# A list scheduler's rules set anew: who holds the port of VectorE and GpSimd, how long dependent operations wait, how long operations last

## The chip, the cores and the metric

The kernel runs on one core of a Trainium2 chip. The core's engines work side by side, each through its own queue in order: TensorE (PE in the profile; its weight loads are PEld), VectorE (DVE), ScalarE (ACT), GpSimd (POOL), and SyncE (SP), which issues the DMAs. The metric is the device time of one execution in microseconds; lower is better. Three runs of the kernel before took 2602.37, 2603.43 and 2603.91 us; the median is 2603.43 us.

## The reference

The input is `x`, 128 graphs of 128 nodes with 256 features in float32, and an adjacency matrix `adj` of 128x128 for each graph. Four layers follow each other, and each ends in `x = layernorm(x + layer(x, adj))` over the features.

Layer 0 is a gated graph network of three steps. In each, a message is formed and summed over the neighbours, and a gated recurrent unit (GRU) takes it in:

```
m = h @ weight[i];  aggr = A^T @ m
r = sigmoid(i_r + h_r);  z = sigmoid(i_z + h_z);  n = tanh(i_n + r * h_n)
h = (1 - z) * n + z * h
```

Here `i_*` are the three parts of `aggr @ w_ih.T + b_ih` and `h_*` those of `h @ w_hh.T + b_hh`. Layers 1 to 3 are graph attention: `Wh = x @ W.T`, `e[i,j] = leaky_relu(Wh[i].a1 + Wh[j].a2, 0.2)`, masked by `adj`, a softmax over `j`, and the result times `Wh`. In layer 2 a node without neighbours gives zero.

## The kernel before, in words

**Tiling.** Four graphs form a group (`G = 4`), so that a tile of 128 partitions holds 512 columns; there are 32 groups. For each group `gru` (L534) records the operations of layer 0 and `gat` (L666) those of the three attention layers. The messages' weights are multiplied into the GRU's input weights, so a step is: sum over the neighbours on PE (L566), evict from PSUM, then the gate products (L508). These use Strassen's scheme with seven products in place of eight: `strassen` (L491) issues the products into three PSUM accumulators of the kind `gate`; ACT copies the intermediate ones out (L574, L578, L581) and DVE adds the parts (`add`, L513). What the scheme needs as moving operands are sums and differences of halves of the hidden state and of the aggregate; `sums` (L468, recorded at L478) makes four of them for each operand, 768 in all, on DVE or on POOL. ACT takes the sigmoids as tanh (L592) and the tanh (L621); DVE combines (L608, L612, L615, L618, L628, L631), and one subtraction (L626) may run on DVE or POOL.

In attention, DVE forms the scores as products with an accumulated row sum (L677), PE turns them into a row (L689), POOL spreads the row over the partitions (`partition_broadcast`, L696), DVE adds the mask and takes the maximum (L712), ACT applies the leaky rectifier (L716) and the exponential (L733), with tiny DVE operations of 128x4 between them (L722, L725, L729). PE transposes the result (L744), it is scaled or evicted (L749 on DVE, L753 on ACT), PE forms the two products (L774, L785), and DVE normalizes and adds the input (L791). ACT squares for the layernorm (L452), further tiny DVE operations follow (L456, L461, L463), POOL raises a 128x4 tile to the power -0.5 (`power`, L425), and ACT scales at the very end (L798). The last four groups make the scores' row on PE (L706) in place of L689 and L696. Where data is transposed by DMA (`turned`, L387), ACT or DVE takes the two halves of each float apart (`APART`, L402) and puts them together again (`TOGETHER`, L397 on ACT, L301 on DVE).

**What sets the order.** Nothing is issued while the operations are recorded. `plan.op` notes each with the engines that may run it and a duration for each, what it reads and writes, and a priority. `Plan.order` (L93) then runs a list scheduler over planned time. An operation becomes ready on an engine once all it depends on is done, plus a delay (`release`, L121 to L126): the producer's `LATENCY` if it ran on another engine, with `MARGIN` of 300 ns more if the consumer is PE; 60 ns on the same engine, 0 on PE. Among the ready operations of an idle engine the one with the lowest priority number goes first. Buffers are slots in pools (`k2` 28, `k4` 18, five `gate` and three `bank` accumulators in PSUM, and so on), and an operation whose buffers have no free slot waits.

**The port.** The scheduler has one resource beside engines and buffers: a port that DVE and POOL share. An operation names in `port` the engines on which it takes it; it then waits until the port is free and holds it for its planned duration. With `BOTH` it takes it on either engine; the default is `("POOL",)`, so every operation that runs on POOL takes it, and a DVE operation takes it only if marked. Of DVE and POOL the one whose first ready operation has the lower priority number is served first (`older`, L152).

The list that the scheduler returns is then issued as it stands. On the chip no planned time holds anything up: an instruction runs when those before it on its engine are done and its inputs are there.

Of the kernel before, what the change touches and what calls it, by code (L numbers as in the profile page):

```python
# [13 lines left out]
ALU = mybir.AluOpType  # L14
AX = mybir.AxisListType

P = 128
# [32 lines left out]
class Plan:  # L50
# [5 lines left out]
    LATENCY = {"PE": 250, "ACT": 220, "DVE": 200, "POOL": 250, "SP": 4000}  # L56
# [11 lines left out]
    def op(self, engines, fn, reads=(), writes=(), prio=0, lag=0, port=("POOL",), start=0, room=()):  # L68
# [24 lines left out]
    def order(self):  # L93
        import heapq
        for o in self.ops:
            o.missing = len(o.deps)
            o.at = {}
            for d in o.deps:
                d.users.append(o)
# [21 lines left out]
        def release(o):  # L121
            for e in o.engines:
                margin = self.MARGIN if e == "PE" else 0
                when = max([t + (margin + self.LATENCY[e2] if e2 != e else 0 if e == "PE" else 60) for e2, t in o.at.items()],
                           default=0)
                heapq.heappush(arrived, (max(when, o.earliest), o.prio, e, o))  # L126
# [4 lines left out]
        while len(done) < len(self.ops):  # L131
# [20 lines left out]
            older = ready["POOL"] and ready["DVE"] and ready["POOL"][0] < ready["DVE"][0]  # L152
            for e in ("PE", "ACT", "SP") + (("POOL", "DVE") if older else ("DVE", "POOL")):
# [51 lines left out]
def adj_resnorm_kernel(  # L205
# [98 lines left out]
    EVICT = {"ACT": 490, "DVE": 600}  # L304
    APART = {"ACT": 960, "DVE": 615}
    TOGETHER = {"ACT": 1075, "DVE": 615}
# [54 lines left out]
    def score_weights(l, prio):  # L361
# [6 lines left out]
        for k in range(KC):  # L368
            st, mv = Buf("st", 6), Buf("mv", G, 2)
            plan.op({"DVE": 330}, lambda e, k=k, st=st: nc.vector.bn_stats(T(st), T(gwT)[:, l, k, :]),  # L370
                    reads=[(gwT, l)], writes=[st], prio=prio)
            plan.op({"DVE": 110}, lambda e, st=st, mv=mv: nc.vector.bn_aggr(T(mv)[:, 0, :], T(st)),
                    reads=[st], writes=[mv], prio=prio)
            plan.op({"DVE": 330}, lambda e, k=k, mv=mv: nc.vector.tensor_scalar(
                T(gwT)[:, l, k, :], T(gwT)[:, l, k, :], T(mv)[:, 0, 0:1], None, op0=ALU.subtract),
                reads=[mv, (gwT, l)], writes=[(gwT, l)], prio=prio)
# [10 lines left out]
    def turned(src, keys, dst, prio):  # L387
# [15 lines left out]
        plan.op({"SP": 1200}, lambda e: nc.sync.dma_start_transpose(  # L403
# [4 lines left out]
    def transposed(src, src_of, prio):  # L408

        res = []  # L410
        for c in range(KC):
# [5 lines left out]
            plan.op({"PE": 440}, fn, reads=[src], writes=[b_], prio=prio)  # L417
# [4 lines left out]
    def power(ve, prio):  # L422

        rstd = Buf("v", G)
        plan.op({"POOL": 1035}, lambda e: nc.gpsimd.tensor_tensor(T(rstd), T(ve), neghalf, ALU.pow),  # L425
                reads=[ve], writes=[rstd], prio=prio)
        return rstd

    def layernorm(y, dst, prio):
        mv, ve, shift = Buf("mv", G, 2), Buf("v", G), Buf("v", G)  # L430
        for b in range(G):
            st = Buf("st", 6)
            plan.op({"DVE": 330}, lambda e, b=b, st=st: nc.vector.bn_stats(T(st), T(y)[:, b, :]),
                    reads=[(y, b)], writes=[st], prio=prio)
            plan.op({"DVE": 110}, lambda e, b=b, st=st: nc.vector.bn_aggr(T(mv)[:, b, :], T(st)),
                    reads=[st], writes=[(mv, b)], prio=prio)
        plan.op({"DVE": 100}, lambda e: nc.vector.tensor_scalar(T(ve), T(mv)[:, :, 1], EPS, None, op0=ALU.add),
                reads=[(mv, b) for b in range(G)], writes=[ve], prio=prio)
        rstd = power(ve, prio)
        plan.op({"DVE": 100}, lambda e: nc.vector.scalar_tensor_tensor(  # L440
            T(shift), T(mv)[:, :, 0], -1.0, T(rstd), op0=ALU.mult, op1=ALU.mult),
            reads=[(mv, b) for b in range(G)] + [rstd], writes=[shift], prio=prio)
        for b in range(G):
            plan.op({"ACT": 415}, lambda e, b=b: nc.scalar.activation(  # L444
# [3 lines left out]
    def deviation(y, before, prio):  # L448

        ss, ve = Buf("v", G), Buf("v", G)  # L450
        for b in range(G):
            plan.op({"ACT": 415}, lambda e, b=b: nc.scalar.activation(  # L452
                next(nobody[0]), T(y)[:, b, :], AF.Square, accum_out=T(ss)[:, b:b + 1]),
                reads=[(y, b)], writes=[(ss, b)], prio=prio)
        if before is None:
            plan.op({"DVE": 100}, lambda e: nc.vector.tensor_scalar(  # L456
                T(ve), T(ss), 1.0 / D, EPS, op0=ALU.mult, op1=ALU.add),
                reads=[(ss, b) for b in range(G)], writes=[ve], prio=prio)
        else:
            eps = Buf("v", G)  # L460
            plan.op({"DVE": 100}, lambda e: nc.vector.tensor_scalar(T(eps), T(before), EPS, None, op0=ALU.mult),  # L461
                    reads=[before], writes=[eps], prio=prio)
            plan.op({"DVE": 100}, lambda e: nc.vector.scalar_tensor_tensor(  # L463
                T(ve), T(ss), 1.0 / D, T(eps), op0=ALU.mult, op1=ALU.add),
                reads=[(ss, b) for b in range(G)] + [eps], writes=[ve], prio=prio)
        return ve

    def sums(ms, prio):  # L468
# [5 lines left out]
        for j, (a, b, reads) in enumerate((  # L474
                (second, first, [ms[0]]), (fourth, part(0), [ms[1], (t, 0)]), (fourth, second, ms),
                (part(1), third, [ms[1], (t, 1)]))):
            plan.op({"POOL": 720, "DVE": 350}, lambda e, j=j, a=a, b=b: (
# [13 lines left out]
    def strassen(gates, kept, prio):  # L491
# [7 lines left out]
        def product(dst, m, first, *room):  # L499
# [10 lines left out]
            plan.op({"PE": 432 * len(todo)}, fn, reads=list(keys), writes=[dst], prio=prio, room=room)  # L510

        def add(b_, part, o, j):
            plan.op({"DVE": 630}, lambda e: nc.vector.tensor_add(  # L513
# [20 lines left out]
    def gru(g, stage):  # L534
# [20 lines left out]
        for i in range(STEPS):  # L555
# [4 lines left out]
            for c in range(KC):  # L560
# [6 lines left out]
                plan.op({"PE": 4 * 222}, fn, reads=[am, xs if h is None else h[c]], writes=[b_], prio=prio, room=[a_])  # L567
# [5 lines left out]
            def whole(dst, src, c):  # L573
                plan.op({"ACT": 500}, lambda e: nc.scalar.copy(T(dst), T(src)),  # L574
                        reads=[src], writes=[(dst, 0), (dst, 1)], prio=prio)

            def halves(dst, src, c):
                plan.op({"ACT": 370}, lambda e: nc.scalar.activation(  # L578
                    T(dst)[:, 0:H], T(src)[:, 0:H], AF.Identity, bias=bhn[:, c:c + 1]),
                    reads=[src], writes=[(dst, 0)], prio=prio)  # L580
                plan.op({"ACT": 260}, lambda e: nc.scalar.copy(T(dst)[:, H:GN], T(src)[:, H:GN]),  # L581
# [5 lines left out]
            for c in range(KC):  # L587
# [6 lines left out]
                for gt in range(2):  # L594
                    if c == 0:
                        plan.op({"ACT": 630}, lambda e, gt=gt, o=o, tanh=tanh: tanh(gt, 0, GN, lambda: T(o)[:, gt, :]),
                                reads=[(o, 0), (o, 1)], writes=[(o, 2 + gt)], prio=prio)
                    else:
                        plan.op({"ACT": 365}, lambda e, gt=gt, tanh=tanh, rz=rz: tanh(
# [4 lines left out]
                if c == 1:  # L604
                    plan.op({"ACT": 370}, lambda e, v=v, nn=nn: nc.scalar.activation(  # L605
                        T(v)[:, 0, 0:H], T(nn[2])[:, 0:H], AF.Identity, bias=bhn[:, 1:2]),
                        reads=[nn[2]], writes=[(v, 0)], prio=prio)
                plan.op({"DVE": 620}, lambda e, o=o, v=v: nc.vector.scalar_tensor_tensor(  # L608
                    T(v)[:, 0, :], T(o)[:, 0, :], 1.0, T(v)[:, 0, :], op0=ALU.add, op1=ALU.mult),
                    reads=[(o, 2), (v, 0), (v, 1)], writes=[(v, 2)], prio=prio, port=BOTH)  # L610
                if c == 0:
                    plan.op({"DVE": 620}, lambda e, v=v: nc.vector.tensor_add(T(v)[:, 0, :], T(v)[:, 1, :], T(v)[:, 0, :]),  # L612
                            reads=[(v, 2)], writes=[(v, 3)], prio=prio, port=BOTH)
                else:
                    plan.op({"DVE": 350}, lambda e, v=v, nn=nn: nc.vector.tensor_add(  # L615
                        T(v)[:, 0, 0:H], T(nn[2])[:, H:GN], T(v)[:, 0, 0:H]),
                        reads=[(v, 2), nn[2]], writes=[(v, 3)], prio=prio)
                    plan.op({"DVE": 350}, lambda e, v=v: nc.vector.tensor_add(  # L618
                        T(v)[:, 0, H:GN], T(v)[:, 1, H:GN], T(v)[:, 0, H:GN]),
                        reads=[(v, 2)], writes=[(v, 4)], prio=prio, port=BOTH)  # L620
                plan.op({"ACT": 630}, lambda e, v=v, c=c: nc.scalar.activation(  # L621
# [3 lines left out]
                plan.op({"POOL": 1250, "DVE": 610}, lambda e, d=d, v=v, h_=hT[c]: (  # L625
                    nc.vector if e == "DVE" else nc.gpsimd).tensor_tensor(T(d), T(h_), T(v)[:, 0, :], ALU.subtract),  # L626
                    reads=[hT[c], (v, 5)], writes=[d], prio=prio, port=BOTH)
                plan.op({"DVE": 620}, lambda e, d=d, o=o: nc.vector.scalar_tensor_tensor(  # L628
                    T(d), T(o)[:, 1, :], 1.0, T(d), op0=ALU.add, op1=ALU.mult),
                    reads=[(o, 3), d], writes=[d], prio=prio, port=BOTH)  # L630
                plan.op({"DVE": 620}, lambda e, d=d, v=v: nc.vector.scalar_tensor_tensor(  # L631
# [10 lines left out]
            for c in range(KC):  # L642
# [8 lines left out]
                plan.op({"PE": 440}, fn, reads=[hT2[c]], writes=[b_], prio=prio)  # L651
                if last:
                    plan.op({"DVE": 620}, lambda e, b_=b_, c=c, y=y: nc.vector.tensor_add(
# [12 lines left out]
    def gat(g, xc, no, stage):  # L666
# [3 lines left out]
        for l in range(3):  # L670
# [4 lines left out]
            for h in (1, 0):  # L675
                for b in range(G):
                    plan.op({"DVE": 345}, lambda e, b=b, h=h, l=l, f=f, xc=xc: nc.vector.scalar_tensor_tensor(  # L677
                        next(nobody[1]), T(xc)[:, b, :], 1.0, T(wa)[:, l, h, :], op0=ALU.mult, op1=ALU.mult,
                        accum_out=T(f)[:, b, 1 - h:2 - h]), reads=[(xc, b), (wa, l)], writes=[(f, 2 * b + h)], prio=prio, port=BOTH)
                if l:  # L680
                    plan.op({"DVE": 100}, lambda e, h=h, f=f, rstd=rstd: nc.vector.tensor_mul(
                        T(f)[:, :, 1 - h], T(f)[:, :, 1 - h], T(rstd)), reads=[(f, 2 * b + h) for b in range(G)] + [rstd],
                        writes=[(f, 2 * b + h) for b in range(G)], prio=prio)
# [3 lines left out]
            if g < NG - LAST:  # L687

                plan.op({"PE": 115}, lambda e, b_=b_, f=f: nc.tensor.transpose(  # L689
# [3 lines left out]
                plan.op({"ACT": 250, "DVE": 200}, lambda e, b_=b_, row=row: copy(e, T(row), T(b_)[:, 0:P]),  # L693
                        reads=[b_], writes=[row], prio=prio)
                for b in range(G):
                    plan.op({"POOL": 300}, lambda e, row=row, b=b, e_=e_: nc.gpsimd.partition_broadcast(  # L696
# [6 lines left out]
            else:  # L703
# [4 lines left out]
                plan.op({"PE": 440}, fn, reads=[(f, 2 * b + 1) for b in range(G)], writes=[b_], prio=prio)  # L708
                rows, keys, port = (lambda b, b_=b_: T(b_)[:, b * P:(b + 1) * P]), lambda b, b_=b_: [b_], ("POOL",)

            for b in range(G):
                plan.op({"DVE": 215}, lambda e, rows=rows, b=b, e_=e_, top=top: nc.vector.tensor_tensor_reduce(  # L712
                    T(e_)[:, b, :], rows(b), T(no)[:, b, :], 1.0, 3 * FAR, ALU.add, ALU.max,
                    T(top)[:, b:b + 1]), reads=keys(b) + [no, (e_, b)], writes=[(e_, b), (top, b)], prio=prio, port=port)
            for b in range(G):
                plan.op({"ACT": 285}, lambda e, b=b, f=f, e_=e_: nc.scalar.activation(  # L716
                    T(e_)[:, b, :], T(e_)[:, b, :], AF.Prelu, bias=T(f)[:, b, 1:2], alpha=SLOPE),
                    reads=[(f, 2 * b), (e_, b)], writes=[(e_, b)], prio=prio)
            if l == 1:

                some = Buf("v", G)
                plan.op({"DVE": 100}, lambda e, some=some, top=top: nc.vector.tensor_scalar(  # L722
                    T(some), T(top), 0.5 * FAR, None, op0=ALU.is_gt),
                    reads=[(top, b) for b in range(G)], writes=[some], prio=prio)
            plan.op({"DVE": 100}, lambda e, f=f, top=top: nc.vector.scalar_tensor_tensor(  # L725
                T(top), T(top), -1.0, T(f)[:, :, 1], op0=ALU.mult, op1=ALU.subtract),
                reads=[(top, b) for b in range(G)] + [(f, 2 * b) for b in range(G)],
                writes=[(top, b) for b in range(G)], prio=prio)
            plan.op({"DVE": 100}, lambda e, top=top, nmax=nmax: nc.vector.scalar_tensor_tensor(  # L729
                T(nmax), T(top), SLOPE, T(top), op0=ALU.mult, op1=ALU.min),  # L730
                reads=[(top, b) for b in range(G)], writes=[nmax], prio=prio)
            for b in range(G):
                plan.op({"ACT": 390}, lambda e, b=b, e_=e_, nmax=nmax, den=den: nc.scalar.activation(  # L733
                    T(e_)[:, b, :], T(e_)[:, b, :], AF.Exp, bias=T(nmax)[:, b:b + 1],
                    accum_out=T(den)[:, b:b + 1]), reads=[(e_, b), nmax], writes=[(e_, b), (den, b)], prio=prio)
# [3 lines left out]
            else:  # L739
# [5 lines left out]
                plan.op({"PE": 440}, fn, reads=[(e_, b) for b in range(G)], writes=[b_], prio=prio)  # L745
                if l:
# [7 lines left out]
                    plan.op({"DVE": 630, "ACT": 1100}, scaled, reads=[b_, rstd], writes=[pT], prio=prio)  # L754
# [105 lines left out]
```

## Time and profile before

| What | Value |
|---|---|
| median of three runs | 2603.43 us |
| span of the profiled execution, first to last instruction | 2600.0 us |
| that execution's own time | not given; its span is 3.4 us under the median |
| PE busy | 2549.3 us, 98% |
| DVE busy | 2124.2 us, 82% |
| ACT busy | 1856.4 us, 71% |
| POOL busy | 601.7 us, 23% |
| sums L478 on DVE (459 and 420 ns each) | 451 |
| sums L478 on POOL (817 and 783 ns each) | 317 |
| mean granted clock of PE | 0.998 |

Busy times are of one execution. An instruction's time in the profile reaches to the end of its writes, so two that follow each other on an engine overlap a little: the pace of an engine is read from the distance of starts. PE's times are modelled and say less than its pace.

### The profile page before, as it was taken

The page shows a single profiled execution, that of the slowest core. Times are in us where ns is not written, and L with a number is a line of the kernel's source. Part 1 is how long each engine was busy: PE and PEld are TensorE (multiplying, and loading weights), DVE is VectorE, ACT ScalarE, POOL GpSimd, SP SyncE. Part 2 cuts the span into 40 slices and gives each one's busy share as a digit, 9 for nine tenths or more (in the row PEclk, how much of TensorE's full clock was granted, in tenths as well). Part 3 has the DMA queues.
Part 4 walks back from the last instruction along what each step waited for, and adds up shares of the span by engine and source line. Part 5 has one row for each costly group of instructions (what it writes and reads, how often), then busy time and mean ns, then how long its engine had stood idle before and what let it go on. Part 6 is the DMA issues. An engine that isn't in the chain of part 4 may idle for free.

```text
span 2600.0 us, 41538 instructions
## 1 busy us (share of the span) xinstructions
PE 2549.3 (98%) x13484; PEld 2257.3 (87%) x13484; DVE 2124.2 (82%) x6262; ACT 1856.4 (71%) x4750; POOL 601.7 (23%) x866
## 2 busy tenths in 40 slices
PE   8999999999999999999999999999999999999988
PEld 7888888888888888888888888888888888888877
DVE  6688888978888888888888888888888887867687
ACT  5667776877778677777777776777786776665467
POOL 2022222322222221222212222212222211322011
PEclk9999999999999999999999999999999999999999
DMA  5211121312122211222121222121222121100001
GB/s 138 61 38 45 38 48 40 72 41 46 41 49 58 48 39 46 49 50 53 41 49 42 53 49 53 42 45 42 49 58 49 37 49 42 21 13 25 17 1 34
DMA packets 281307, 117.79 MB, mean 45 GB/s; under 512 B 213888, under 2 KB 279424, under 8 KB 281088
## 3 DMA queue, kind: packets, MB, share of 16 engines
q1 hardware_dynamic: 280656, 115.12, 19.1%
q8 instruction: 106, 1.74, 0.3%
q14 instruction: 113, 0.93, 0.1%
q10 hardware_dynamic: 432, 0.01, 0.0%
HBM read 45.89 MB, written 16.78 MB: 24 GB/s over the span
## 4 chain that ended last, share of the span: by engine, by line
PE 82%; DVE 10%; ACT 4%; issue 2%; DMA 1%; POOL 0%; POOLq 0%; ACTq 0%; SPq 0%; DVEq 0%
PE gate L508 59%; PE bank L785 11%; PE bank L774 6%; PE bank L566 4%; DVE k L712 2%; ACT k L733 2%; DVE nobody L677 1%; PE bank L650 1%; DVE k L513 1%; DVE k L301 1%; DVE k L791 1%; PE bank L744 1%; ACT k L299 1%; DVE v L729 1%; DVE v L722 1%
## 5 line engine op out<-in xcount | busy, mean ns | idle before, releaser
L508 PE MATMUL gate<-k,whs 128*128 128x256 f32 x4032 | 1203.3, 380 | 18.1 <-ACT k L574 15.8
L508 PE MATMUL gate<-k,wcs 128*128 128x256 f32 x4032 | 1199.3, 379 | 0.0
L508 PEld LDWEIGHTS gate<-k,wcs 128*128 128x128 f32 x4032 | 766.0, 190 | 104.2 <-issue 0.2
L508 PEld LDWEIGHTS gate<-k,whs 128*128 128x128 f32 x4032 | 736.5, 190 | 115.5 <-ACT k L574 22.5
L513 DVE TENSOR_TENSOR k<-gate,k 128x512 f32<-128x512 f32 x576 | 390.3, 684 | 145.3 <-PE gate L508 124.0
L785 PE MATMUL bank<-gwT,k 128*128 128x256 f32 x1536 | 348.7, 380 | 1.3 <-DVE k L301 1.2
L785 PEld LDWEIGHTS bank<-gwT,k 128*128 128x128 f32 x1536 | 290.5, 190 | 42.4 <-DVE k L301 2.9
L677 DVE SCALAR_TENSOR_TENSOR nobody<-k,wa 128x256 f32<-128x256 f32 x768 | 293.7, 428 | 23.1 <-ACT k L444 21.7
L425 POOL TENSOR_TENSOR v<-v,neghalf 128x4 f32<-128x4 f32 x128 | 136.0, 1062 | 731.8 <-DVE v L463 375.7
L452 ACT ACTIVATE nobody<-k 128x256 f32<-128x256 f32 x384 | 156.2, 408 | 193.2 <-DVE k L791 192.3
L299 ACT COPY k<-bank 128x512 f32<-128x512 f32 (+1 forms) x314 | 177.0, 566 | 136.9 <-PE bank L566 79.2
L397 ACT COPY k<-k 128x1024 uint16<-128x1024 uint16 x182 | 209.1, 1159 | 80.3 <-DMA k<-k 76.0
L592 ACT ACTIVATE k<-k,brz 128x256 f32<-128x256 f32 (+1 forms) x384 | 225.1, 627 | 42.4 <-DVE k L513 42.4
L791 DVE SCALAR_TENSOR_TENSOR k<-bank,v,k 128x256 f32<-128x256 f32 x384 | 167.5, 477 | 81.6 <-PE bank L785 81.3
L626 POOL TENSOR_TENSOR k<-k,k 128x512 f32<-128x512 f32 x79 | 101.3, 1282 | 506.8 <-issue 297.3
L574 ACT COPY k<-gate 128x512 f32<-128x512 f32 x288 | 166.2, 587 | 71.3 <-PE gate L508 70.7
L478 POOL TENSOR_TENSOR k<-k,k 128x256 f32<-128x256 f32 x215 | 172.2, 817 | 164.5 <-ACT k L299 69.5
L774 PEld LDWEIGHTS bank<-k,k 128*128 128x128 f32 x1536 | 188.1, 193 | 12.9 <-DVE k L791 2.1
L774 PE MATMUL bank<-k,k 128*128 128x128 f32 x1536 | 191.1, 277 | 4.8 <-DVE k L791 1.7
L733 ACT ACTIVATE k<-k,v 128x128 f32<-128x128 f32 x384 | 149.5, 397 | 47.7 <-DVE v L729 47.4
L696 POOL PARTITION_BROADCAST k<-k x336 | 114.1, 439 | 230.3 <-issue 111.2
L608 DVE SCALAR_TENSOR_TENSOR k<-k,k 128x512 f32<-128x512 f32 x192 | 148.6, 783 | 20.9 <-ACT k L605 20.3
(97 smaller groups left out, 3238.1 us busy)
## 6 DMA issues: line engine op xcount, KB each, us to landing
xs<-in_x_dram SPq DMA_DIRECT2D x32, 512.0 KB, 3.9
k<-in_x_dram SPq DMA_DIRECT2D x32, 512.0 KB, 4.1
out_dram<-k SPq DMA_DIRECT2D x32, 512.0 KB, 2.9
am<-in_adj_dram SPq DMA_DIRECT2D x32, 256.0 KB, 2.9
k<-k SPq DMA_TRANSPOSE x200, 3.1
k<-in_gnn_wT_dram SPq DMA_DIRECT2D x3, 256.0 KB, 5.0
k<-in_w_ihT_dram SPq DMA_DIRECT2D x2, 384.0 KB, 5.9
k<-in_w_hhT_dram SPq DMA_DIRECT2D x2, 384.0 KB, 6.1
```

Of the source, the lines that this page charges most:

```text
L299: nc.scalar.copy(dst, src)
L397: nc.scalar.copy(flat().bitcast(U16).rearrange("p (q h) -> p q h", h=2), T(rows).bitcast(U16).rearrange("p (h q) -> p q h", h=2))
L478: nc.vector if e == "DVE" else nc.gpsimd).tensor_tensor(T(t)[:, j, :], a(), b(), ALU.subtract),
L508: nc.tensor.matmul(T(dst)[:, j * H:(j + 1) * H], T(w)[:, m, gt, :], moving(m, ms)[1](), start=first and n == 0, stop=n == len(todo) - 1, s ...
L513: plan.op({"DVE": 630}, lambda e: nc.vector.tensor_add(T(o)[:, :, j * H:(j + 1) * H], T(b_).rearrange("p (g n) -> p g n", g=2), T(part).re ...
L574: plan.op({"ACT": 500}, lambda e: nc.scalar.copy(T(dst), T(src)), reads=[src], writes=[(dst, 0), (dst, 1)], prio=prio)
L592: nc.scalar.activation(T(o)[:, gt, n0:n1], src(), AF.Tanh, bias=brz[:, gt * KC + c:gt * KC + c + 1], scale=0.5)
L677: plan.op({"DVE": 345}, lambda e, b=b, h=h, l=l, f=f, xc=xc: nc.vector.scalar_tensor_tensor(next(nobody[1]), T(xc)[:, b, :], 1.0, T(wa)[:, ...
L733: plan.op({"ACT": 390}, lambda e, b=b, e_=e_, nmax=nmax, den=den: nc.scalar.activation(T(e_)[:, b, :], T(e_)[:, b, :], AF.Exp, bias=T(nmax ...
L774: nc.tensor.matmul(T(b_)[:, b * P:(b + 1) * P], T(xc)[:, b, c * P:(c + 1) * P], T(pT)[:, b, :], start=True, stop=True)
L785: nc.tensor.matmul(T(b_)[:, (b - b0) * D:(b - b0 + 1) * D], T(aT[k])[:, b * P:(b + 1) * P], T(gwT)[:, l, k, :], start=(k == 0), stop=(k == ...
L791: nc.vector.scalar_tensor_tensor(T(y)[:, b, :], T(b_)[:, (b - b0) * D:(b - b0 + 1) * D], T(rden)[:, b:b + 1], T(xc)[:, b, :], op0=ALU.mult ...
```

## The change

All operations stay, with their arithmetic. New are the planner's rules and numbers.

The delay between dependent operations comes from a table by producer and consumer engine, `DELAY`; what it lacks comes from `LATENCY`, whose values are smaller. On one engine the delay is now 145 ns for ACT, 120 for DVE and 115 for POOL (60 before). `MARGIN` is added wherever a PE operation depends on another engine, as before.

The default of `port` is empty: the powers, the broadcasts and the library load on POOL no longer take the port, nor do DVE operations that were left to the default. Most of the tiny 128x4 DVE operations are marked `BOTH`, so they wait while POOL holds the port and hold it themselves for 78 ns. Sums and the subtraction L626 take it as before. Of DVE and POOL the one that has waited longer, or will have been able to start earlier, is served first (`waited`).

The durations are set anew, mostly 10 to 30 ns lower; some rise (L444 from 415 to 491, L791 from 340 to 393, the transposing DMA from 1200 to 1285). Operations with an accumulated output get a `lag`, 75 ns on DVE and 85 on ACT, that delays those who read them. The diff, cut to its kinds:

```diff
-    LATENCY = {"PE": 250, "ACT": 220, "DVE": 200, "POOL": 250, "SP": 4000}
+    LATENCY = {"PE": 220, "ACT": 190, "DVE": 165, "POOL": 120, "SP": 4000}
+
+    DELAY = {("PE", "PE"): 0, ("PE", "ACT"): 210, ("PE", "DVE"): 210, ("ACT", "PE"): 165, ("ACT", "DVE"): 145,
+             ("ACT", "POOL"): 190, ("ACT", "ACT"): 145, ("DVE", "PE"): 140, ("DVE", "ACT"): 120, ("DVE", "POOL"): 165,
+             ("DVE", "DVE"): 120, ("POOL", "POOL"): 115, ("POOL", "ACT"): 95, ("POOL", "DVE"): 95}
...
-    def op(self, engines, fn, reads=(), writes=(), prio=0, lag=0, port=("POOL",), start=0, room=()):
+    def op(self, engines, fn, reads=(), writes=(), prio=0, lag=0, port=(), start=0, room=()):
...
-            o.at = {}
+            o.at, o.when = {}, {}
...
-                when = max([t + (margin + self.LATENCY[e2] if e2 != e else 0 if e == "PE" else 60) for e2, t in o.at.items()],
+                when = max([t + self.DELAY.get((e2, e), self.LATENCY[e2]) + (margin if e2 != e else 0) for e2, t in o.at.items()],
                            default=0)
+                o.when[e] = max(when, o.earliest)
...
-            older = ready["POOL"] and ready["DVE"] and ready["POOL"][0] < ready["DVE"][0]
-            for e in ("PE", "ACT", "SP") + (("POOL", "DVE") if older else ("DVE", "POOL")):
+            waited = {e: max(idle[e], min((i[1].when[e] for i in ready[e] if i[1] not in started), default=now)) for e in ("POOL", "DVE")}
+            for e in ("PE", "ACT", "SP") + (("POOL", "DVE") if waited["POOL"] < waited["DVE"] else ("DVE", "POOL")):
...
-    EVICT = {"ACT": 490, "DVE": 600}
-    APART = {"ACT": 960, "DVE": 615}
-    TOGETHER = {"ACT": 1075, "DVE": 615}
+    EVICT = {"ACT": 475, "DVE": 602}
+    APART = {"ACT": 938, "DVE": 602}
+    TOGETHER = {"ACT": 1058, "DVE": 602}
...
-        plan.op({"POOL": 1035}, lambda e: nc.gpsimd.tensor_tensor(T(rstd), T(ve), neghalf, ALU.pow),
+        plan.op({"POOL": 980}, lambda e: nc.gpsimd.tensor_tensor(T(rstd), T(ve), neghalf, ALU.pow),
...
-            plan.op({"POOL": 720, "DVE": 350}, lambda e, j=j, a=a, b=b: (
+            plan.op({"POOL": 690, "DVE": 335}, lambda e, j=j, a=a, b=b: (
...
-            plan.op({"DVE": 630}, lambda e: nc.vector.tensor_add(
+            plan.op({"DVE": 602}, lambda e: nc.vector.tensor_add(
...
-                plan.op({"ACT": 500}, lambda e: nc.scalar.copy(T(dst), T(src)),
+                plan.op({"ACT": 475}, lambda e: nc.scalar.copy(T(dst), T(src)),
...
-                plan.op({"POOL": 1250, "DVE": 610}, lambda e, d=d, v=v, h_=hT[c]: (
+                plan.op({"POOL": 1235, "DVE": 602}, lambda e, d=d, v=v, h_=hT[c]: (
...
-                    plan.op({"DVE": 100}, lambda e, h=h, f=f, rstd=rstd: nc.vector.tensor_mul(
+                    plan.op({"DVE": 78}, lambda e, h=h, f=f, rstd=rstd: nc.vector.tensor_mul(
                         T(f)[:, :, 1 - h], T(f)[:, :, 1 - h], T(rstd)), reads=[(f, 2 * b + h) for b in range(G)] + [rstd],
-                        writes=[(f, 2 * b + h) for b in range(G)], prio=prio)
+                        writes=[(f, 2 * b + h) for b in range(G)], prio=prio, port=BOTH)
...
-                plan.op({"ACT": 390}, lambda e, b=b, e_=e_, nmax=nmax, den=den: nc.scalar.activation(
+                plan.op({"ACT": 385}, lambda e, b=b, e_=e_, nmax=nmax, den=den: nc.scalar.activation(
                     T(e_)[:, b, :], T(e_)[:, b, :], AF.Exp, bias=T(nmax)[:, b:b + 1],
-                    accum_out=T(den)[:, b:b + 1]), reads=[(e_, b), nmax], writes=[(e_, b), (den, b)], prio=prio)
+                    accum_out=T(den)[:, b:b + 1]), reads=[(e_, b), nmax], writes=[(e_, b), (den, b)], prio=prio, lag=85)
```

## The prediction

> **What bounds the kernel now.** I read the page's busy shares first, then the chain that ended last, then who made TensorE (PE) wait, then one repeating stretch in order of time, and last the busy times of the end.
>
> ```profile
> PE 2549.3 (98%) x13484; PEld 2257.3 (87%) x13484; DVE 2124.2 (82%) x6262; ACT 1856.4 (71%) x4750; POOL 601.7 (23%) x866
> ...
> PE 82%; DVE 10%; ACT 4%; issue 2%; DMA 1%; POOL 0%; POOLq 0%; ACTq 0%; SPq 0%; DVEq 0%
> ```
>
> PE is the bound. A busy PE is not a PE at its peak, so I rebuild its least time from the pace of its records. The chain in order of time repeats itself:
>
> ```profile
> 934.71 10.36 PE gate L508 x48
> 945.18 12.09 PE gate L508 x56
> ...
> 1013.56 10.36 PE gate L508 x48
> 1024.04 12.09 PE gate L508 x56
> ```
>
> Two things are to be seen. 12.09 us for 56 records is 0.216 us for a 256-wide record; the other pieces of the chain give 0.1115 us for a 128-wide product record and 0.109 us for a transpose. And the pattern returns after 78.85 us: one group of four graphs. A group's PE work is 252 L508 and 48 L785 records x 0.216, 96 (L774, L566) x 0.1115, 19 transposes x 0.109: 64.8 + 10.7 + 2.1 = 77.55 us. So 1.30 us of each group is standstill. Over the program, 8064 + 1536 wide, 3072 narrow and 740 transpose records, with some 21 us for the weights, need 2517 us; PE starts at 5.2 and begins its last record at 2591.2, so about 69 us are standstill. L508's last record ends at 2502.1. Behind it lie 71.2 us of PE work (by the order of the instructions), so 18 us of the standstill are in the end part and 51 before it. Of these 51, 26 us (20 groups x 1.30) lie between 600 and 2200 us; the rest is at the start and around 400 to 600 and 2200 to 2500.
>
> Where the 1.30 us comes from, in order of time, one group:
>
> ```profile
> 971.60 4.01 POOL L478 TENSOR_TENSOR k<-k,k 128x256 f32<-128x256 f32 x5
> ...
> 972.41 0.28 DVE L712 CUSTOM_DVE_ANT_0 k<-k,am 128x128 f32<-128x128 f32 x1
> ...
> 972.62 0.80 DVE L712 CUSTOM_DVE_ANT_0 k<-k,am 128x128 f32<-128x128 f32 x1
> ...
> 974.95 0.68 DVE L722 TENSOR_SCALAR v<-v 128x4 f32<-128x4 f32 x1
> ...
> 976.31 0.73 POOL L478 TENSOR_TENSOR k<-k 128x256 f32<-128x256 f32 x1 [0.70 <-DVE v L725]
> 976.33 0.72 DVE L729 SCALAR_TENSOR_TENSOR v<-v 128x4 f32<-128x4 f32 x1
> ...
> 977.15 0.40 ACT L733 ACTIVATE k<-k,v 128x128 f32<-128x128 f32 x1 [2.18 <-DVE v L729]
> ...
> 978.18 1.01 PE L744 MATMUL bank<-ident,k 128*128 128x128 f32 x4
> ...
> 979.81 0.70 PE L508 MATMUL gate<-k,whs 128*128 128x256 f32 x2 [0.62 <-ACT k L574]
> ```
>
> While POOL works through sums (L478), VectorE's (DVE's) two-input L712 takes 0.80 instead of 0.28, and the tiny L722 and L729 take 0.68 and 0.72 (a tiny one undisturbed takes about 0.16). DVE loses some 3 us, ScalarE (ACT) waits 2.18 us for L729, its exponentials come late, PE's transposes L744 take 1.01 instead of 0.60, and ACT's copy L574, queued behind the exponentials, holds the next product up for 0.62. The old rules do not see this: the tiny operations ask for no port.
>
> A second place shows what does not collide:
>
> ```profile
> 496.57 1.01 POOL L425 TENSOR_TENSOR v<-v,neghalf 128x4 f32<-128x4 f32 x1
> ...
> 496.98 0.41 DVE L677 SCALAR_TENSOR_TENSOR nobody<-k,wa 128x256 f32<-128x256 f32 x1
> ...
> 497.55 0.73 POOL L478 TENSOR_TENSOR k<-k,k 128x256 f32<-128x256 f32 x1
> 497.62 0.68 DVE L681 TENSOR_TENSOR f<-f,v 128x4 f32<-128x4 f32 x1 [0.22 <-POOL v L425]
> ```
>
> Beside POOL's power (L425) the two-input L677 takes its usual 0.41; beside a sum even the tiny L681 takes 0.68. The old rules keep DVE's port operations away from powers and broadcasts too.
>
> **The change, part by part.** No operation is added; its places and engines are planned anew. By the order of the instructions on each engine, of the 768 sums POOL takes 596 instead of 317, and of the 192 subtractions L626, 86 instead of 79. DVE hands off 286 of these, 24 interleaving copies net and 13 small copies, and takes 23 more each of 128x512 bank copies and L749; at the rows' means DVE's work falls by about 121 us, POOL's rises by 235, ACT's falls by 24. SP issues the same 343 instructions, its transposes planned 85 ns longer.
>
> *Durations and delays.* The new durations are close to the pace in the trace: consecutive 128x512 DVE operations of the chain come every 0.60 (L628: 1.20 for two; planned 602), exponentials every 0.39 (planned 385, was 390), the four L798 take 1.70 in all (planned 400 each, was 500). Truer numbers cost nothing by themselves. What they take away is cover: a product behind an ACT copy was planned 490+220+300 = 1010 ns after the copy's start and is now 475+165+300 = 940; the row above has L574 at 979.18 and its product at 979.81, 0.63 us. The cover shrinks from 0.38 to 0.31 us. PE's 300 ns stay, so I cost this at nothing; were the cover gone, each of the some 50 waits for L574 would grow by at most 0.07, 3.5 us.
>
> *The port rules.* Tiny operations now wait for the port in the plan, powers and broadcasts no longer take it, and of DVE and POOL the one that has waited longer goes first. If the plan meets the clash of 971 to 980 us, the 1.30 us go. Ends: all gone, -26 us; or clashes in proportion to POOL's sums (596/317 = 1.88), so 0.88 x 26 = +23 us. I take -20, 0.3 us left per group, since the rows show each kind of clash where the new rules put it and none where they drop it. Of the other 25 us before the last L508, whose waits are of the same kinds, I take a third: -8 (ends -16 and +12).
>
> A page of the Trainium skill speaks against half of this: "SBUF — State Buffer", section "Who interferes with whom", lets a GpSimd instruction that reads SBUF lock the pair against any DVE operation with two SBUF inputs, for its whole length. A power reads SBUF, so by that rule 128 x 1.06 = 136 us of DVE could be blocked, and in the DVE-bound end 13 powers would cost some 14 us. The row of 496.98 us (0.41 beside a power) says nothing is lost; I go by the row.
>
> *The sums on POOL.* A sum takes 771 to 817 ns there and 416 to 459 on DVE: 0.355 us longer, for 279 moved sums 99 us of latency. Queued behind them are the first products of each step (they read the last sum) and POOL's own powers and broadcasts, for which ACT's L798 and DVE's L712 wait. What hides it: PE has another group's products at hand. The waits of PE name no POOL at all with 317 sums there, so I take 0 of the 99; the other end is all 99.
>
> *The end part.* There DVE is the bound:
>
> ```profile
> 2500.00:2520.00 20.00, 15.35 (x87) 12.26 (x85) 19.49 (x86) 14.95 (x51) 6.01 (x5) 0.97 0.00 1
> ...
> 2540.00:2560.00 20.00, 18.12 (x112) 15.89 (x110) 19.75 (x116) 17.05 (x73) 3.21 (x3) 1.00 0.00 1
> ```
>
> The third busy time is DVE's: 19.5 and 19.75 of 20 us. After the last gate addition (L513) the old order leaves DVE 87.6 us (76 L677 x 0.345, 88 L712 x 0.212, 48 L791 x 0.393, 14 copies, some 85 small ones and a few more), the new one 91.1 (80 L677, 94 L712, 15 copies): +3.5 us (ends -3, a shorter chain behind the powers, and +8).
>
> **The sum.** -20 - 8 + 0 + 3.5 = -24.5 us. The profiled execution's span is 2600.0, 3.4 us under the median of 2603.4 (its own time is not given). So 2575.5 of span, 2579 us of time.
>
> **The rivals.** (1) *PE starves for sums.* POOL's sums, with the port held 0.69 us each, delay the first products. At 25% of the 99 us on PE's path the gain is gone; at 40% the time is 2579 + 40 = 2619. For it: three quarters of all sums, up to four in a row of 0.77 us, must now pass POOL before a product. Against it: no PE wait names POOL. (2) *The clash only moves.* POOL with nearly twice the sums meets other DVE operations; the 1.30 us per group stay at another place: -4 + 3.5, so 2603. For it: in order of time POOL runs as soon as its inputs are there, whatever the plan meant. (3) *All standstill before the end goes*: -51 + 3.5, about 2556. For it: PE works in other groups without any gap for 70 us on end; against it: the start waits for loads (5.2 us on x alone).
>
> **How the numbers follow.** Mine 0.43, (1) 0.22, (2) 0.15, (3) 0.20. The range must reach (3) and most of (1): 2556 to 2618; mine alone spans 2568 to 2590. A difference under 0.2% (5.2 us) can't be told from none. Faster: mine, (3) and a third of (2), 0.68; same: 0.08, most of (2); slower: (1) and the rest, 0.24.
>
> **What would show it.** Right: the pattern in L508's chain returns after about 77.9 us per group; L722, L729, L681 and L712 near their undisturbed 0.16 and 0.28; POOL busy about 837 us; ACT's wait for L729 (47.4 us) mostly gone; DVE near 2000 us. Wrong: a PE wait for POOL's L478, DVE's L478, L608 or L677 longer than now, or an end part more than 8 us longer.

## The result and the profile after

The changed kernel takes 2575.95 us (median of 4 runs, 2574.74 to 2577.16) against 2602.9 us (4 runs) before: a ratio of 0.9897, 95% interval [0.9883, 0.9911], 27 us less. Forecast were 2579 us. The span of the profiled execution fell from 2600.0 to 2575.3 us; the mean granted clock of PE is 0.998 in both. The kernel's lines named here moved down by 5 (L508 is L513 now, L574 L579, L729 L734). The busy times of the page:

```profile
PE 2538.2 (99%) x13484; PEld 2253.5 (88%) x13484; DVE 2070.5 (80%) x5985; ACT 1854.4 (72%) x4672; POOL 884.1 (34%) x1152
...
PE 88%; DVE 6%; ACT 3%; issue 2%; DMA 1%; POOL 1%; POOLq 0%; ACTq 0%; SPq 0%; DVEq 0%
```

PE's share of the chain that ended last rose from 82% to 88%, those of DVE and ACT fell. In that chain, in order of time (start, length), the pattern now returns every five groups:

```profile
709.43 12.09 PE gate L513 x56
...
1100.14 12.09 PE gate L513 x56
...
1490.55 12.09 PE gate L513 x56
...
1881.53 12.09 PE gate L513 x56
```

1881.53 - 709.43 is 1172.1 us for 15 groups: 78.14 us a group against 78.85 before. With 77.55 us of work, 0.59 us of a group are standstill, 1.30 before.

What PE waited for between 200 and 2200 us, first before, then after (total us, times, longest):

```profile
PE gate L508 <- ACT k L574: 11.6, 19, 0.6
PE bank L689 <- DVE f L681: 2.2, 2, 1.1
```

```profile
PE bank L694 <- DVE nobody L682: 5.2, 6, 1.0
PE bank L779 <- DVE k L306: 1.4, 1, 1.4
...
PE gate L513 <- ACT k L579: 0.5, 1, 0.5
```

The wait for the copy behind the exponentials, 19 times in some 25 groups before, is listed once. The end part, after the change (window, its length, then busy PE, PEld, DVE, ACT, POOL):

```profile
2475.00:2500.00 25.00, 19.97 (x112) 16.97 (x110) 22.95 (x112) 19.54 (x68) 4.87 (x5) 0.86 0.00 1
2500.00:2520.00 20.00, 17.07 (x102) 14.76 (x103) 20.00 (x123) 16.21 (x67) 2.89 (x3) 1.00 0.00 1
2520.00:2540.00 20.00, 19.35 (x124) 16.86 (x123) 20.00 (x117) 17.04 (x73) 3.18 (x3) 1.00 0.01 2
```

From 2500 to 2540 us DVE is full, as before.

For all kernels below I add up PE's standstill in one way: the distance between the starts of successive PE records, less the undisturbed step of the same kind, all from the one profiled execution of each kernel. Where the 24.7 us of span come from:

| us | before | after | difference |
|---|---|---|---|
| standstill, 0 to 200 us | 5.6 | 5.6 | 0 |
| standstill, 200 to 2200 us ("steady") | 36.3 | 21.4 | -14.9 |
| standstill, 2200 us to the last L508 or L513 ("change-over") | 10.5 | 1.3 | -9.2 |
| PE work behind that product | 71.1 | 73.3 | -2.2 ahead of it |
| from that product to the end of the span ("end") | 98.3 | 99.9 | +1.6 |

In the steady part PE began 10503 records before and 10600 after (the first x below), which points the same way without my sum; the granted clock, third from the right, is 1.00 in both:

```profile
200.00:2200.00 2000.00, 1981.03 (x10503) 1761.46 (x10502) 1671.27 (x4923) 1469.57 (x3764) 481.23 (x715) 1.00 0.20 46
```

```profile
200.00:2200.00 2000.00, 1989.37 (x10600) 1772.09 (x10599) 1642.39 (x4754) 1492.48 (x3733) 711.66 (x955) 1.00 0.21 48
```

### The profile page after: what moved, and what is told of

Its sections match the earlier page's. It is cut to its first block, busy times and chain, and to the rows that moved or that the text cites. A ratio compares the mean times of both kernels' runs of the same rounds, so it can differ in the third digit from the quotient of the medians.

```text
span 2575.3 us, 41426 instructions
## 1 busy us (share of the span) xinstructions
PE 2538.2 (99%) x13484; PEld 2253.5 (88%) x13484; DVE 2070.5 (80%) x5985; ACT 1854.4 (72%) x4672; POOL 884.1 (34%) x1152
## 4 chain that ended last, share of the span: by engine, by line
PE 88%; DVE 6%; ACT 3%; issue 2%; DMA 1%; POOL 1%; POOLq 0%; ACTq 0%; SPq 0%; DVEq 0%
PE gate L513 61%; PE bank L790 11%; PE bank L779 6%; PE bank L571 6%; DVE nobody L682 2%; PE bank L655 1%; PE bank L749 1%; DVE k L518 1%; DVE k L796 1%; DMA k<-k 1%; DVE k L717 1%; ACT k L304 1%; DVE k L613 1%; PE bank L694 0%; DMA am<-in_adj_dram 0%
## 5 line engine op out<-in xcount | busy, mean ns | idle before, releaser
L513 PE MATMUL gate<-k,whs 128*128 128x256 f32 x4032 | 1201.5, 380 | 3.7 <-DVE k L518 1.4
L513 PE MATMUL gate<-k,wcs 128*128 128x256 f32 x4032 | 1199.2, 379 | 0.0
L513 PEld LDWEIGHTS gate<-k,wcs 128*128 128x128 f32 x4032 | 766.0, 190 | 104.3 <-issue 0.3
L513 PEld LDWEIGHTS gate<-k,whs 128*128 128x128 f32 x4032 | 738.6, 190 | 96.1 <-ACT k L579 4.4
L518 DVE TENSOR_TENSOR k<-gate,k 128x512 f32<-128x512 f32 x576 | 392.0, 685 | 174.9 <-PE gate L513 140.1
L483 POOL TENSOR_TENSOR k<-k,k 128x256 f32<-128x256 f32 x453 | 378.3, 854 | 288.1 <-DVE k L636 128.4
L682 DVE SCALAR_TENSOR_TENSOR nobody<-k,wa 128x256 f32<-128x256 f32 x768 | 298.7, 435 | 6.7 <-ACT k L449 3.1
L304 ACT COPY k<-bank 128x512 f32<-128x512 f32 (+1 forms) x304 | 167.2, 554 | 118.7 <-PE bank L571 41.7
L579 ACT COPY k<-gate 128x512 f32<-128x512 f32 x288 | 164.4, 579 | 109.0 <-PE gate L513 107.3
L631 POOL TENSOR_TENSOR k<-k,k 128x512 f32<-128x512 f32 x86 | 112.1, 1304 | 313.4 <-ACT k L626 255.9
L626 ACT ACTIVATE k<-k,bi 128x512 f32<-128x512 f32 x192 | 137.9, 722 | 87.6 <-DVE k L623 46.8
L483 POOL TENSOR_TENSOR k<-k 128x256 f32<-128x256 f32 x143 | 126.8, 890 | 215.6 <-DVE k L636 125.1
L402 ACT COPY k<-k 128x1024 uint16<-128x1024 uint16 x147 | 170.2, 1167 | 38.6 <-DMA k<-k 38.0
L701 POOL PARTITION_BROADCAST k<-k x336 | 132.0, 493 | 156.8 <-DVE k L306 87.1
```

The costliest lines, as they stand in the source:

```text
L304: nc.scalar.copy(dst, src)
L402: nc.scalar.copy(flat().bitcast(U16).rearrange("p (q h) -> p q h", h=2), T(rows).bitcast(U16).rearrange("p (h q) -> p q h", h=2))
L483: nc.vector if e == "DVE" else nc.gpsimd).tensor_tensor(T(t)[:, j, :], a(), b(), ALU.subtract),
L513: nc.tensor.matmul(T(dst)[:, j * H:(j + 1) * H], T(w)[:, m, gt, :], moving(m, ms)[1](), start=first and n == 0, stop=n == len(todo) - 1, s ...
L518: plan.op({"DVE": 602}, lambda e: nc.vector.tensor_add(T(o)[:, :, j * H:(j + 1) * H], T(b_).rearrange("p (g n) -> p g n", g=2), T(part).re ...
L579: plan.op({"ACT": 475}, lambda e: nc.scalar.copy(T(dst), T(src)), reads=[src], writes=[(dst, 0), (dst, 1)], prio=prio)
```

## The experiments

The change has three parts: the port rules (P), the delays (L), and the durations (T). The theories at the start: A, the port rules remove the clash, as I predicted; B, truer durations and delays let the plan fit the chip; C, the order is a lottery. All kernels were timed in three rounds against the kernel before.

**One part alone, and a nudge.** e1 puts P alone into the kernel before, e2 T alone, e3 L alone with the lags; e4 is

```diff
-    MARGIN = 300
+    MARGIN = 320
```

> The kernel before with the port rules alone: default port empty, the 11 marked kinds of tiny operations with port BOTH, and the longest-waiting engine first; durations and delays as before. Theory A (the port rules remove the clash that made the exponentials late): most of the 27 us, 2603 - 20 = about 2583 us, and the standstill per group in L508's chain under 0.5 us. Theory B (truer durations and delays let the plan fit the chip): about 2600, at most 8 us of gain. Theory C (any nudge of the plan lands somewhere between 2570 and 2630 by chance): no firm number.

> The kernel before with the new durations alone; delays and port rules as before. Theory A: 2603 within 5 us, the clash at the exponentials stays at about 1.3 us per group. Theory B: at least half of the gain, 2590 or less. Theory C: no firm number.

> The kernel before with the new delays alone (LATENCY, DELAY, the lags of accumulated outputs); durations and port rules as before. Theory A: 2603 within 5 us. Theory B: with the durations it makes up the gain, so 2590 here or in the run with the durations. Theory C: no firm number.

> The kernel before with MARGIN 320 in place of 300, nothing else: a nudge that by itself should be worth nothing. Theories A and B: 2603 within 5 us. Theory C (the order is a lottery): a change of 10 us or more either way.

| kernel | us | ratio to before | steady | change-over | end |
|---|---|---|---|---|---|
| e1, P | 2607.5 | 1.0022 [1.0013, 1.0032] | 44.8 | 4.7 | 103.8 |
| e2, T | 2638.0 | 1.0137 [1.0120, 1.0154] | 74.0 | 10.2 | 98.3 |
| e3, L | 2611.9 | 1.0035 [1.0022, 1.0048] | 44.8 | 8.0 | 104.5 |
| e4, nudge of before | 2616.5 | 1.0054 [1.0039, 1.0069] | 37.0 | 25.2 | 102.6 |

No part gains anything alone. Theory A falls as stated, and so does B for either of its halves. Under this nudge the steady part stays (36.3 and 37.0), while the change-over and the end lose 19 us. So times alone can't judge an edit of this size here; the steady standstill is the better measure.

The clash itself has to be told apart from the gain. The table shows ACT's wait for L729 between 200 and 2200 us, the mean lengths of the three tiny operations ahead of the exponentials, and the steady standstill split in two: at the transposes L744 and the product behind them, where the prediction saw the clash, and elsewhere. e6, e8 and e10 are told of below; all lines are named as in the kernel before.

| kernel | ACT waits for L729, us | L722, L725, L729, ns | standstill at L744 and behind it | elsewhere |
|---|---|---|---|---|
| before | 44.3 | 505, 196, 287 | 24.3 | 12.0 |
| after, P L T | 26.6 | 301, 327, 214 | 0.0 | 21.4 |
| e1, P | 6.1 | 253, 259, 183 | 0.0 | 44.8 |
| e2, T | 9.6 | 199, 188, 189 | 2.2 | 71.8 |
| e3, L | 25.1 | 308, 201, 248 | 15.0 | 29.8 |
| e6, L T | 52.8 | 556, 184, 310 | 11.8 | 32.9 |
| e8, P L | 4.5 | 282, 236, 217 | 0.0 | 22.9 |
| e10, tiny unmarked | 19.3 | 179, 192, 188 | 0.3 | 41.7 |

P alone does clear the place that the prediction named: 24.3 us go there. But 32.8 us more come up elsewhere, at PE's waits for other copies and evictions. The waits of before, e1 and e6 in order (total us, times, longest):

```profile
ACT k L733 <- DVE v L729: 44.3, 23, 2.5
```

```profile
ACT k L734 <- DVE v L730: 6.1, 9, 1.7
```

```profile
ACT k L738 <- DVE v L734: 52.8, 25, 2.2
```

**One part undone, and the nudge of the changed kernel.** e5 has MARGIN 320 in the changed kernel, e6 lacks P, e7 lacks L, e8 lacks T.

> The changed kernel with MARGIN 320 in place of 300, nothing else. Theory B2 (the gain comes from a plan whose rules, delays and durations are all true together; the steady part keeps to it): the standstill of the steady part, 200 to 2200 us, stays near 21 us, and the time stays under 2590. Theory C (the order is a lottery, and the changed kernel drew well): 2595 or more, as the same nudge of the kernel before cost 13.6 us.

> The changed kernel with the old port rules: new durations and delays together, powers and broadcasts take the port again, tiny operations do not, the lower priority number first. Theory B2: the clash comes back, 2600 or more, with a standstill of the steady part over 35 us. Theory D (durations and delays belong together, since a shorter duration needs the longer delay on the same engine; the port rules matter little): 2585 or less. Theory C: anything between 2575 and 2640.

> The changed kernel with the old delays: new durations and port rules. Theory B2: 2600 or more. Theory D: about as slow as the durations alone, 2625 or more, since dependent operations on one engine are planned 60 ns apart where 120 to 145 are needed. Theory C: anything between 2575 and 2640.

> The changed kernel with the old durations: new delays and port rules. Theory B2: 2590 or more, a steady standstill above 30 us. Theory D: 2605 or more, as with the delays alone (2612). Theory C: anything between 2575 and 2640.

| kernel | us | ratio to before | steady | change-over | end |
|---|---|---|---|---|---|
| after, P L T | 2576.0 | 0.9897 [0.9883, 0.9911] | 21.4 | 1.3 | 99.9 |
| e5, nudge of after | 2594.0 | 0.9965 [0.9952, 0.9978] | 26.6 | 5.4 | 108.6 |
| e6, L T | 2617.3 | 1.0053 [1.0038, 1.0068] | 44.7 | 14.0 | 99.5 |
| e7, P T | 2635.8 | 1.0127 [1.0112, 1.0142] | 68.4 | 2.6 | 108.8 |
| e8, P L | 2593.9 | 0.9965 [0.9951, 0.9979] | 22.9 | 3.7 | 109.1 |

The steady column has a clear rule. With port rules and delays together it is 21 to 27, with or without new durations; with no part at all 36 to 37; with one of P and L but not the other 45; and 68 to 74 where the new durations stand on the old delays, with P or without. So P and L gain only together, T gains nothing in the steady part, and T without L costs 24 to 38. That is theory B2 less its durations: e8 stayed at 22.9, not above 30. The two nudges moved this column by 0.7 and 5.2, which is its noise as far as it was tried; why P and L need each other was not followed through the plan. e5 lies between the bounds of both theories (2590 and 2595): of its 18 us, 5 are in the steady part and the rest behind it. Between the two nudged kernels lie 22.5 us, between the two as given 27.

For theory C there remains the end. The changed kernel's change-over and end take 101.2 us together; its near neighbours e5 and e8 take 114.0 and 112.8. Some 12 us of the result are a good draw of this order, as those of before (108.8 against 127.8 in e4) were.

**The port rules one by one, and the kind of delay.** From the changed kernel: e9 has the old turn (`older`), e10 the 11 kinds of tiny operations unmarked, e11 the old default. e12 has

```diff
-                when = max([t + self.DELAY.get((e2, e), self.LATENCY[e2]) + (margin if e2 != e else 0) for e2, t in o.at.items()],
+                when = max([t + (self.DELAY.get((e2, e), self.LATENCY[e2]) + margin if e2 != e else 0 if e == "PE" else 60) for e2, t in o.at.items()],
```

> The changed kernel with the old turn between DVE and POOL (lower priority number first); empty default and marked tiny operations stay. Standstill of the steady part, 200 to 2200 us, is 21 in the changed kernel and 36 in the one before. If the turn is what counts (the plan gives the port to the engine that has waited, as the chip does): 35 or more. If it is not: 21 to 27. The time also carries the end part, which moved by 9 us under a nudge, so the steady standstill decides.

> The changed kernel with the 11 kinds of tiny DVE operations unmarked again, so the plan puts them beside POOL's sums. The step of the prediction (the clash of the tiny operations is what made the exponentials late): steady standstill 35 or more. If the tiny operations don't count: 21 to 27, though more of them are blocked.

> The changed kernel with the old default: powers and broadcasts take the port in the plan again. They don't collide on the chip, so this only holds DVE back in the plan for some 230 us of port time that is free. If this matters: steady standstill 30 or more. If not: 21 to 27.

> The changed kernel with 60 ns between dependent operations of one engine again (0 on PE), the new delays between engines kept. If the longer delay on one engine is what the shorter durations need: steady standstill 60 or more, as without any of the new delays (68). If the delays between engines are the ones that count: 21 to 30.

| kernel | us | ratio to before | steady | sums on POOL | DVE blocked |
|---|---|---|---|---|---|
| before | 2602.9 | | 36.3 | 317 | 133 |
| after | 2576.0 | 0.9897 [0.9883, 0.9911] | 21.4 | 596 | 152 |
| e9, old turn | 2634.8 | 1.0121 [1.0104, 1.0137] | 65.6 | 267 | 94 |
| e10, tiny unmarked | 2605.7 | 1.0007 [0.9997, 1.0016] | 42.0 | 575 | 162 |
| e11, old default | 2675.4 | 1.0278 [1.0263, 1.0294] | 109.0 | 680 | 173 |
| e12, 60 ns on one engine | 2586.7 | 0.9938 [0.9923, 0.9953] | 23.7 | 598 | 165 |

"DVE blocked" is what DVE's instructions took over the lower quartile of their group, where that is more than 40 ns. All three port rules are needed: each one undone by itself costs more than the whole gain of the steady part. Each is one order, though, and one nudge of this kernel cost 5.2. In e10 a wait with the name of my prediction's is back (PE between 200 and 2200 us):

```profile
PE gate L513 <- ACT k L579: 6.9, 17, 1.9
PE bank L694 <- DVE nobody L682: 6.3, 14, 0.5
```

It is another wait. In e10 the three tiny operations ahead of the exponentials are undisturbed (179, 192 and 188 ns), and nothing is lost at the transposes behind the exponentials (0.3 us in the table above). PE stands at the scores' row (L694) and at the product that follows it, 27.8 us in the steady part. One such place, in order of time:

```profile
633.00 1.42 POOL L631 TENSOR_TENSOR k<-k,k 128x512 f32<-128x512 f32 x1 [0.34 <-DVE nobody L682]
...
633.22 1.48 DVE L682 SCALAR_TENSOR_TENSOR nobody<-k,wa 128x256 f32<-128x256 f32 x1
...
634.63 0.94 DVE L682 SCALAR_TENSOR_TENSOR nobody<-k,wa 128x256 f32<-128x256 f32 x1
...
635.73 0.30 PE L694 MATMUL bank<-ident,f 128*128 128x128 f32 x1 [0.46 <-ACT k L304]
...
636.18 0.70 PE L513 MATMUL gate<-k,whs 128*128 128x256 f32 x2 [0.16 <-ACT k L579]
```

The scores L682, which kept their mark, take 1.48 and 0.94 us beside POOL. So e10 shows that the marks matter, but not by the clash at the exponentials. In e11 PE waits for the same scores, which it is to turn into a row:

```profile
PE bank L694 <- DVE nobody L682: 48.9, 18, 3.6
```

48.9 us in 18 waits make up over half of the 87.6 us that it lost in the steady part; 25 us more are records at half the clock behind such waits (last section). That planned port time for powers and broadcasts keeps L682 late is argued from the edit; I did not follow it through the plan. e12 refutes the ground that I had given for e7 and for theory D: the longer delay on one engine is not what the shorter durations need. What counts is in the rest of L, since e12 keeps it and stays at 23.7, and e7 keeps none of it and has 68.4. That rest is the delays between engines, the lags, and the smaller `LATENCY`, which also sets when the plan frees a buffer's slot. Which of the three, and which pair of engines, was not tried.

## Why the prediction was right, and where its reasons were not

*The bound and the place.* Right: PE is the bound, and in the kernel before 24.3 of the 36.3 us of steady standstill lie at the transposes L744 and the product behind them. After the change nothing is lost there, and the wait of PE for L574 went from 11.6 to 0.5 us.

*The port rules, -20 us by themselves.* The size was near (I left 0.3 us per group, 0.59 remain: -14 in place of -20), but crediting it to P alone failed. "The rows show each kind of clash where the new rules put it and none where they drop it" led me there. e1, with P alone, clears the place (24.3 to 0.0) and gains nothing, since PE stands elsewhere (12.0 to 44.8); after the whole change it is 21.4 elsewhere. Nor does the place need P's marks: it stays empty in e10, and nearly so with T alone (2.2 in e2), both without a gain.

*Durations and delays, costed at nothing.* This step failed. I bounded it by PE's cover (0.38 to 0.31 us) and 3.5 us. Leaving the new delays out costs 60 us (e7), 47 of them steady. By the code, delays also decide which operation the planner takes next on every engine, not only how much cover PE has; that this is where the 47 us come from is my reading and was not traced. For the durations "nothing" holds in the steady part, provided the delays are new (e8).

*The rest before the last product, -8 us.* Measured -9.2 in the change-over, and -0.9 us in what of the steady part is not in the groups' pattern. The number fits, but a nudge of either kernel moves this part by 4 to 15 us; it was luck that it fits.

*The end part, +3.5 us.* Measured +1.6 with 2.2 us more PE work behind the last product. DVE is full, as I said, but the order alone moves the end by 9 us (e5).

*The sum.* 24.7 us of span against 24.5 forecast is in part luck: -14 for -20 in the groups, -10 for -8 in the rest, and -0.6 (1.6 - 2.2) for +3.5 at the end cancel. The step from span to time was wrong too: I added 3.4 us, where time is 1.7 to 2.1 us over the span in every run listed since.

*The sums on POOL, 0 of 99 us.* Right: no wait of PE names POOL in the trace after.

*The rivals.* (1) did not occur. (2) is half true: the clash did move. The groups of instructions after the change (count, busy us, mean ns of one, then idle time before them):

```profile
L483 POOL TENSOR_TENSOR k<-k,k 128x256 f32<-128x256 f32 x453 | 378.3, 854 | 288.1 <-DVE k L636 128.4 <-ACT k L304 64.2 <-DVE k L306 27.7
...
L483 DVE TENSOR_TENSOR k<-k,k 128x256 f32<-128x256 f32 x123 | 75.6, 618 | 5.7 <-ACT k L304 1.1 <-POOL k L483 0.6 <-ACT k L402 0.2
...
L730 DVE SCALAR_TENSOR_TENSOR v<-v,f 128x4 f32<-128x4 f32 x96 | 31.3, 327 | 1.5
...
L686 DVE TENSOR_TENSOR f<-f,v 128x4 f32<-128x4 f32 x128 | 25.5, 212 | 12.0 <-PE bank L694 5.9 <-POOL v L430 5.6
...
L734 DVE SCALAR_TENSOR_TENSOR v<-v 128x4 f32<-128x4 f32 x96 | 20.4, 214 | 1.4
...
L727 DVE TENSOR_SCALAR v<-v 128x4 f32<-128x4 f32 x32 | 9.6, 301 | 0.4
```

My signs said that L722, L729, L681 and L712 would be near 0.16 and 0.28. They fell from 505, 287, 279 and 364 ns to 301, 214, 212 and 341, no further; L725 rose from 196 to 327, the sums left on DVE from 459 to 618, those on POOL from 817 to 854. POOL is busy 884 us and not 837, DVE 2070 and not near 2000, and DVE's blocked time rose from 133 to 152 us. ACT's wait for L729 fell only from 47.4 to 31.3 over the whole span. (3) did not occur: 28 of the 52 us before the last product remain.

The blocked time does not tell the time at all: e9 has the least of it (94 us) and a steady standstill of 65.6, three times that of the changed kernel. What seems to count is whose clash it is, and whether PE has other work at that moment; no run tests that by itself.

## What to carry to other kernels

In a list scheduler with several rules, a rule that is truer by itself can make the order worse: try the rules together and each undone, and don't credit the one whose mechanism the trace shows best, even where its wait does go away. A wait that comes back under the same name can have another cause: look at what stands ahead of it. Before a gain of 1% is ascribed to a rule, nudge an idle number of the plan in both kernels, and compare the repeating part by PE's standstill per group, apart from the start and the end. Busy time lost to a port says little while the bound engine has other work.

## What the runs showed of the hardware

*A power beside DVE costs nothing.* In the trace after, 111 of the two-input L682 began while POOL was already in a power, and met nothing else there: they took 420 ns in the mean, as did those with an idle POOL. The Trainium skill ("SBUF — State Buffer", section "Who interferes with whom") would have them blocked for the power's whole length; the measurement decides. For the sums it holds: L717 takes 0.81 us beside one in place of 0.28. It also holds that an operation with one input in PSUM is free: 107 gate additions L518 beside a sum that was already running took 686 ns in the mean, 330 beside nothing 685.

*A broadcast does collide, a little.* I had taken broadcasts to be free. The changed kernel plans DVE's L613 beside them, DVE and POOL in order of time:

```profile
345.64 2.04 POOL L701 PARTITION_BROADCAST k<-k  x4 [1.16 <-PE bank L694]
...
346.62 0.77 DVE L613 SCALAR_TENSOR_TENSOR k<-k,k 128x512 f32<-128x512 f32 x1
...
347.76 0.86 POOL L483 TENSOR_TENSOR k<-k 128x256 f32<-128x256 f32 x1
...
347.97 0.81 DVE L717 CUSTOM_DVE_ANT_0 k<-k,am 128x128 f32<-128x128 f32 x1
```

L613 takes 0.77 us (0.69 undisturbed), and the four broadcasts 2.04 us, where they took 1.33 us at 970.18 us of the trace before: the first, beside the end of a DVE operation L636, takes 0.73 in place of 0.43, and the last, which starts while L613 runs, 0.83. In all 15 cases of L613 beside broadcasts alone it took 0.77 to 0.79.

*A long pause of PE is followed by half its clock.* In e11's steady part the granted clock is 0.50 in 14 stretches of 3.4 or 6.8 us; 13 of them begin at the end of a long pause, where two successive PE records start 3.6 to 4.0 us apart. Inside them a 256-wide record takes 0.427 us in place of 0.216, and records at such a doubled step add up to 25.4 of the 109.0 us of steady standstill. One stretch (the clock third from the right):

```profile
1129.40:1136.10 6.70, 5.93 (x18) 4.96 (x19) 4.95 (x16) 4.34 (x6) 5.77 (x11) 0.50 0.78 159
```

In the steady part of the kernels before and after there is none, and taken off they leave the groups of the steady column as they are (e2 65.5, e7 65.6, e9 60.2, e11 83.6). In e4 they make up 7.6 of the 14.7 us by which the change-over grew.

*A plan's nudge is worth 14 to 18 us.* 20 ns more of a margin moved the time by 0.5% and 0.7%. In the kernel before nearly all of it lay behind 2200 us, where the last groups overlap in another way; in the changed kernel 5 of the 18 us lay in the steady part.
